# Three causal tiles in flight and context attention tile by tile in the first block, with interleaved queries in the second, of a four-block Perceiver kernel

## The chip, the core and the metric

One core of a Trainium2 chip runs the whole program. The metric is device microseconds of one execution, the median of the runs shown. Everything is float32. The engines are named as the profile names them: PE (TensorE matmul; PEld is its weight load), DVE (VectorE), ACT (ScalarE), POOL (GpSimd) and SP (SyncE, which issues most of the DMA transfers).

## The reference, cut to what matters

The network takes `x` (16 batches, 64 tokens, 256 features) and a context (16 batches, 1024 tokens, 192 features) through four blocks. Each block is a cross-attention on the context, a mixer over the tokens, and a feed-forward part, each added to `x` after a layer norm. The change touches the first block's first two parts and the second block's first part:

```python
x = x + L0_xattn(layernorm(x), ctx)      # one wide head: softmax(q k^T / 16) v, no output projection
x = x + L0_attn(layernorm(x), ...)       # rms-normed q, k; 16 heads of 16, causal over the 64 tokens
x = x + L0_ffn(layernorm(x), ...)        # top-2 of 8 experts, plus one shared expert
x = x + L1_xattn(layernorm(x), ctx)      # 16 heads of 16 on the context ("narrow heads")
...
```

## The kernel before, in words

The 1024 tokens are 8 tiles of 128 (two batches each), held in `xs`. A tile framework puts the instructions of each engine in an order and places the waits; inside `manual_schedule(engines={PE})` the PE's instructions keep the order in which the Python code emits them. The engines run their own lists in order, so an instruction that waits holds up all that stands behind it on its engine.

**First block, `L0_first`.** Per tile `i`, `scores(i)` multiplies queries that already carry the key weights (`qp`) with the transposed context (`ctxT`) of two batches into a PSUM tile `sc` of two banks; `exp_rows` takes the row maximum on DVE (`nmx`, L223) and the exponential on ACT (`p`, L225). `keys_first` turns `p` round on the PE (`ps_t`, L235) and copies it to `pT`. `averaged` multiplies `pT` with the context tokens (`ctx`, L349) and divides (`on`, L250). `by_features` transposes the result (L359, L360, copies `onT`), and `output` multiplies by the value weights (`misc<-w,onT`) and adds to `xs`. These run as a software pipeline over three iterations of the loop `for n in range(NT + 2)`: in iteration `n` the scores are those of tile `n`, the transposes and averages those of tile `n-1`, the output that of tile `n-2`.

Between these pieces stand nine calls of `attn.go()` per iteration. Each call advances the generators of `causal_attention`: every causal tile that is in flight (two at most) does its next piece, and so does the first routing generator in the list `behind`. A causal tile has 19 yields, many of them empty pieces that only leave time. In order its pieces are: the norm of `xs` (`os`); its transposes (`hTs`); the q, k, v matmuls (`misc<-w,hTs`) with the rms norm; transposes of q and k (`pt`, L717); scores of all heads (`sc<-w`), whose two PSUM tiles take both `sc` buffers, the mask (`sm`, L741), maxima (`mx`), a subtraction on POOL (L748), `exp` (L749), sums (L750); transposes of the exponentials (`pt`, L756); the products with v (`o`, L778, again in an `sc` buffer); the spreading of the sums' reciprocals (`misc<-rT,sel`); the projection (`misc<-w,yT`). A causal tile may start only once the context output of its tokens is in `xs` (`attn.ready`). After two causal tiles their routing for the experts follows. When the loop ends, `attn.go()` is called until all is done, with one piece of the shared expert (`shared_part`, tiles `gu` and `hid`) after each call.

The PSUM tags of this block are `sc` (2 buffers of two banks), `t` (2 of one bank) and `misc` (2 of one bank). Four context buffers hold two tiles' context. Transfers stand in SP's queue in program order; a transfer into a buffer that is still read holds up those behind it. The rooms of the two causal tiles in flight are carved from one slot of a ring of weight buffers.

**Second block, `L1_xattn`.** Per batch `keys_values(b)` gives four pieces (two of keys, two of values); `queries(i)`, in three turns, fetches for one tile of tokens the outputs of their two experts from memory (`carry`: two gathers on POOL, L1375, and two additions on DVE, L1384), normalizes (`ln_rs` on POOL, L160; `o`, L886), transposes, and multiplies, and copies the queries to a second layout by DMA (`qs<-qs`). Steps `(b, g)` then each do the scores, exponentials, transposes and averages of four heads (two score tiles of 128 rows: two heads times 64 queries), the transposes and averages one step behind the scores. Before, a block with PE and DVE in written order does the four pieces of batch 0 and then all of `queries(0)` and `queries(1)`, ahead of the first step:

```python
for piece in keys_values(0):
    piece()
for i in range(2):
    for _ in queries(i):
        pass
```

Of the kernel before, what the change touches and what calls it, by code (L numbers as in the profile page):

```python
# [21 lines left out]
NT = T // 128  # L22
# [20 lines left out]
class Net:  # L43
# [227 lines left out]
    def pack_L0_room(self):  # L271


        self.slot()
        return [
            (
                self.carve(128, 2, 2, 2 * S), self.carve(128, 2, 128), self.carve(128, D), self.carve(128, 2, D),
                self.carve(128, 2, 8, S), [self.carve(128, 4, 128) for _ in range(2)],
            )
            for _ in range(2)  # L280
        ]

    def L0_first(self):
# [5 lines left out]
        self.spare_dve = True  # L289
        self.tag, self.tag_bufs = "t", 2  # L290
        self.more_ctx(self.lp)
        self.norm_x()
# [9 lines left out]
        with self.tc.manual_schedule(engines={mybir.EngineType.PE}):  # L302
# [21 lines left out]
            def scores(i):  # L324
                ctx = ctxs.pop(i) if i in ctxs else fetch(i)
                if i == 2:
                    self.gate_w = self.load("L0f_gateT")
                    self.shared = tuple(self.load(f"L0f_{n}") for n in ("sw1", "sw3", "sw2"))
                sc = self.lps.tile([128, KEYS], F32, tag="sc", bufs=2, name="sc")

                for kh in range(2):
                    keys = bass.ts(kh, 512)
                    for ch in range(2):
                        for par in range(2):
                            b = 2 * i + par
                            nc.tensor.matmul(
                                sc[64 * par : 64 * par + 64, keys], qp[: HC + ch, ch, b * S : (b + 1) * S],
                                ctx[par][0][: HC + ch, ch, keys], start=ch == 0, stop=ch == 1,
                            )
# [30 lines left out]

            held = tail = None
            for n in range(NT + 2):
                got = (n, *scores(n)) if n < NT else None
                attn.go()
                if tail is not None:
                    onT = by_features(tail[1])
                attn.go()
                if held is not None:
                    i, ctx, sums, p = held
                    pT = self.keys_first(p, attn.go)  # L380
                attn.go()
                if tail is not None:
                    output(tail[0], onT)
                    attn.ready = tail[0] + 1
                attn.go()
                tail = None
                if held is not None:
                    tail = i, averaged(i, ctx, sums, pT)
                attn.go()
                attn.go()  # L390
                held = got
            del self.ctxT[2:], self.ctx[2:]
# [270 lines left out]
    def causal_attention(self, wqkv, wproj):  # L663
# [23 lines left out]
        def tile(i):  # L687
            if not rooms:
                rooms.extend(self.pack(ahead=False))
            qs, kT, v, qk, p16, p16T = rooms[i % 2]  # L690
            qs = qs.rearrange("p c b (h q) -> p c b h q", h=2)
            o = normalized(i, sb.tile([128, D], F32, tag="os", bufs=2, name="os"))
            yield
            yield
            hT = sb.tile([128, 2, 128], F32, tag="hTs", bufs=2, name="hTs")
            self.evict(hT, self.transposed(o))
# [3 lines left out]
            self.mm(ps.rearrange("p a b -> p (a b)"), [(hT[:, c, :], wqkv[:, c, :512]) for c in range(2)])  # L700
            sq = sb.tile([128, D], F32, tag="sq", bufs=2, name="sq")
            ss = self.small.tile([128, 2], F32, name="ss")
# [34 lines left out]

            sums = sb.tile([128, 2, 8], F32, tag="sums", bufs=2, name="sums")
            for jp in range(2):
# [21 lines left out]

            r = sb.tile([128, 2, 8], F32, tag="r", bufs=2, name="r")
            nc.vector.reciprocal(
# [4 lines left out]
            for b in range(2):  # L768
                nc.tensor.transpose(pr[:, b, :], r[:, b, :], self.ident)
            rT = sb.tile([8, 2, 128], F32, tag="rT", bufs=2, name="rT")  # L770
            nc.scalar.copy(rT, pr)
# [11 lines left out]
            o = o[:, :, : 4 * S].rearrange("p r (c n) -> p r c n", c=2)  # L783
            ym = sb.tile([128, 2, 2, S], F32, tag="ym", bufs=2, name="ym")
            nc.vector.tensor_scalar(ym, o[:, :, :, :S], own[:, 0:1], None, ALU.mult)
# [6 lines left out]
            for c in range(2):  # L792
                self.mm(ps[:, c], [(sel[:, h, c, :], rT[:, :, 64 * h : 64 * h + 64]) for h in range(2)])
            yT = sb.tile([128, 2, 2, S], F32, tag="yT", bufs=2, name="yT")
            nc.vector.tensor_tensor(
# [34 lines left out]
        def go():  # L830

            if len(s.work) < 2 and s.next < s.ready:
                s.work.append(tile(s.next))
                s.next += 1
            for w in list(s.work):
                if next(w, s) is s:
                    s.work.remove(w)
            if s.behind and next(s.behind[0], s) is s:
                s.behind.pop(0)
            return s.work or s.next < NT or s.behind  # L840
# [8 lines left out]
    def L1_xattn(self):  # L849
# [160 lines left out]
        with self.tc.manual_schedule(engines={mybir.EngineType.PE, mybir.EngineType.DVE}):  # L1010
            biases()
            for piece in keys_values(0):
                piece()
            for i in range(2):
                for _ in queries(i):
                    pass
        with self.tc.manual_schedule(engines={mybir.EngineType.PE}):
            held, work = None, {}
            steps = [(b, g) for b in range(B) for g in range(4)]
            for k in range(len(steps) + 4):  # L1020
# [5 lines left out]
                if k < len(steps):  # L1026
                    b, g = steps[k]
                    if not g:
                        sums = self.lp.tile([128, 8], F32, tag="sums", bufs=3, name="sums")
                        more = keys_values(b + 1) if b + 1 < B else None  # L1030
                    now = (b, g, scores(b, g, sums), sums)
                for piece in work.pop((k, "early"), ()):
                    piece()
                if k < len(steps):
                    if not b % 2 and not g and b // 2 + 2 < NT:
                        ahead = queries(b // 2 + 2)
                    if more is not None:
                        more[g]()
                    if b % 2 == 0 and g < 3 and b // 2 + 2 < NT:
                        next(ahead)  # L1040
# [170 lines left out]
    def shared_part(self, k):  # L1211
# [3 lines left out]
        cols = bass.ts(k, CHUNK)  # L1215
        hid = self.lp.tile([128, 3, CHUNK], F32, tag="hid1", bufs=3, name="hid")
        for m in range(3):
# [14 lines left out]
    def L0_ffn(self):  # L1232
        nc = self.nc
        self.blocks(self.routed, L0_BLOCKS)
        self.tag, self.tag_bufs = "gu", 4
        for k in range(2, NC):
            for _ in self.shared_part(k):
# [1255 lines left out]
```

## Time and profile before

| | before |
|---|---|
| median of 3 runs | 2849.67 us (2848.07 to 2859.1) |
| profiled execution | 2852.74 us, its span 2851.0 us |
| mean granted TensorE clock | 0.959 |
| busy share of the span | PE 92%, PEld 66%, DVE 49%, ACT 35%, POOL 11% |
| first scores of the first block to its last routing matmul | 31.46 to 273.68 us |
| second block's first matmul to its first turned exponentials | 440.18 to 484.25 us |

A page of the profile gives busy time by engine, slices of the span, the chain of work that ended last, the groups of instructions by line, and the waits. The trace answers the same for any stretch of time; "the windows" are a table with one row for each stretch: its length, the busy time of PE, PEld, DVE, ACT and POOL with numbers of instructions, the granted clock, the busy share of the DMA engines and their GB/s. In a timeline a row is start, duration, engine, line, operation, tiles, count, and in brackets the idle time before it with what ended it. Line 69 is the helper `mm`, line 64 the helper `evict`: there the tiles tell which call it is. One matmul of the program is two rows in the trace, since the count of float32 matmuls in the profile is twice that of the code.

### The profile page before, as it was taken

The numbers are of one execution on the slowest core, as the hardware profiler recorded it, in microseconds if no ns is written. First come the engines' busy times: TensorE is split into PE (matmuls) and PEld (weight loads), VectorE is DVE, ScalarE is ACT, GpSimd is POOL, SyncE is SP. The second block draws the span as 40 slices with busy tenths as digits, with TensorE's granted clock in tenths as the row PEclk, the third lists the DMA queues.
The fourth block names the chain that finished last, engine by engine and source line by source line (L and its number), as shares of the span: only waits on it lengthen the run. The fifth ranks groups of instructions, "written<-read, shape, count | busy, mean of one in ns | idle before, by whom it ended". The sixth has DMA issues, their size and how long they took to land.

```text
span 2851.0 us, 44735 instructions
## 1 busy us (share of the span) xinstructions
PE 2610.3 (92%) x18116; PEld 1892.4 (66%) x18116; DVE 1400.3 (49%) x2825; ACT 998.3 (35%) x2110; POOL 312.8 (11%) x429
## 2 busy tenths in 40 slices
PE   7887997999999898979999999698999998998999
PEld 3556894666666586856666676596666566666777
DVE  2655224666666653233434342422344756658692
ACT  1322222555555441222322322122234545454330
POOL 1111333000000011310101000201001000000000
PEclk9987997999999997989999999799999999999999
DMA  8611871110010113811111111463112213121210
GB/s 239 177 50 63 340 279 53 34 35 27 27 38 23 42 38 135 313 54 49 47 54 56 58 49 56 175 239 112 52 49 88 87 49 97 56 75 30 60 45 8
DMA packets 79228, 253.71 MB, mean 89 GB/s; under 512 B 15151, under 2 KB 26954, under 8 KB 69290
## 3 DMA queue, kind: packets, MB, share of 16 engines
q1 hardware_dynamic: 59562, 165.01, 18.3%
q0 software_dynamic: 13312, 80.28, 7.8%
q10 hardware_dynamic: 6144, 5.51, 0.6%
q8 instruction: 145, 2.38, 0.3%
q14 instruction: 65, 0.53, 0.1%
HBM read 233.80 MB, written 14.82 MB: 87 GB/s over the span
## 4 chain that ended last, share of the span: by engine, by line
PE 38%; DVE 9%; ACT 3%; issue 3%; DMA 2%; POOL 1%; SPq 1%; DVEq 0%; POOLq 0%; ACTq 0%
PE sc L501 9%; PE ps_h L69 4%; PE misc L537 4%; PE halves L69 3%; PE misc L69 3%; PE ps_t L515 3%; PE halves L537 3%; PE misc L532 2%; PE gu L69 2%; DVE x L2093 2%; PE halves L2117 2%; PE halves L532 1%; DVE nmx L223 1%; DVE x L2089 1%; DMA rep<-dus 1%
## 5 line engine op out<-in xcount | busy, mean ns | idle before, releaser
L223 DVE TENSOR_REDUCE nmx<-sc 128x1 f32<-128x1024 f32 x264 | 311.7, 1218 | 236.0 <-PE sc L501 146.1
L225 ACT ACTIVATE p<-sc,nmx 128x1024 f32<-128x1024 f32 x264 | 294.3, 1115 | 323.2 <-DVE nmx L223 323.0
L501 PE MATMUL sc<-ctxT,qp 128*128 128x512 f32 (+1 forms) x1024 | 358.3, 604 | 0.0
L501 PEld LDWEIGHTS sc<-ctxT,qp 128*128 128x128 f32 (+1 forms) x1024 | 139.8, 190 | 155.6 <-issue 153.2
L515 PE MATMUL ps_t<-ident,p 128*128 128x128 f32 x1024 | 140.9, 280 | 39.5 <-ACT pT L518 17.0
L2083 ACT ACTIVATE da<-rep,al 128x252 f32<-128x252 f32 x256 | 115.9, 500 | 134.0 <-DVE x L2093 123.8
L515 PEld LDWEIGHTS ps_t<-ident,p 128*128 128x128 f32 x1024 | 115.9, 143 | 64.3 <-ACT pT L518 20.2
L2093 DVE TENSOR_TENSOR_SCAN x<-da,x 128x512 f32<-128x512 f32 x128 | 152.7, 1218 | 2.7 <-ACT da L2083 1.9
L235 PE MATMUL misc<-ident,p 128*128 128x128 f32 x1024 | 137.1, 279 | 9.1 <-ACT p L225 6.3
L518 ACT COPY pT<-ps_t 128x512 f32<-128x512 f32 x166 | 94.2, 587 | 122.1 <-PE ps_t L515 117.1
L235 PEld LDWEIGHTS misc<-ident,p 128*128 128x128 f32 x1024 | 110.1, 141 | 34.8 <-ACT p L225 14.2
L160 POOL TENSOR_TENSOR ln_rs<-ln_ve,nhalf 128x1 f32<-128x1 f32 x80 | 45.1, 571 | 698.0 <-DVE ln_ve L158 605.3
L537 PE MATMUL halves<-pT,ctx 128*128 128x256 f32 x512 | 119.7, 387 | 0.0
L537 PE MATMUL misc<-pT,ctx 128*128 128x256 f32 x512 | 119.1, 386 | 0.0
L2089 DVE TENSOR_TENSOR x<-rep,bc_rep 128x512 f32<-128x512 f32 x128 | 84.6, 687 | 59.9 <-PE halves L2117 57.1
L237 ACT COPY pT<-misc 128x512 f32<-128x512 f32 x128 | 75.0, 586 | 109.7 <-PE misc L235 109.3
L69 PE MATMUL ps_h<-r,w 128*128 128x256 f32 x512 | 113.4, 381 | 0.0
L239 DVE COPY pT<-misc 128x512 f32<-128x512 f32 x128 | 88.3, 690 | 40.3 <-PE misc L235 28.8
L69 PEld LDWEIGHTS ps_h<-r,w 128*128 128x128 f32 x512 | 96.6, 190 | 15.9 <-issue 2.5
L537 PEld LDWEIGHTS halves<-pT,ctx 128*128 128x128 f32 x512 | 95.1, 191 | 17.4 <-issue 5.6
L537 PEld LDWEIGHTS misc<-pT,ctx 128*128 128x128 f32 x512 | 94.6, 190 | 17.1 <-issue 5.5
L69 PE MATMUL po<-wb,hid 128*128 128x256 f32 x440 | 100.3, 379 | 0.0
(500 smaller groups left out, 4502.4 us busy)
## 6 DMA issues: line engine op xcount, KB each, us to landing
ctx<-in_ctx SPq DMA_DIRECT2D x48, 768.0 KB, 4.4
ctxT<-in_ctxT SPq DMA_DIRECT2D x48, 512.0 KB, 3.3
w<-in_L2f_W SPq DMA_DIRECT2D x24, 1024.0 KB, 8.0
rep<-dus SPq DMA_DIRECT2D x256, 64.0 KB, 2.0
ctxT<-in_ctxT SPq DMA_DIRECT2D x16, 768.0 KB, 12.3
ctxT<-in_ctxT SPq DMA_DIRECT2D x96, 128.0 KB, 3.2
ys<-yb ACTq DMA_DIRECT2D x40, 128.0 KB, 7.2
bc_rep<-bcs SPq DMA_DIRECT2D x32, 128.0 KB, 2.9
```

The source lines that it names most:

```text
L69: self.nc.tensor.matmul(out, lhsT, rhs, start=n == 0, stop=n == len(pairs) - 1)
L223: self.nc.vector.tensor_reduce(nmx, sc, AX.X, ALU.max, negate=True)
L225: self.nc.scalar.activation(p, sc, AF.Exp, bias=nmx, accum_out=sums)
L235: self.nc.tensor.transpose(ps[:, u, :], p[:, at : at + 128], self.ident)
L239: self.nc.vector.tensor_copy(pT[:, 0:4, :], ps)
L501: nc.tensor.matmul(sc[u][:, bass.ts(kh, 512)], qp[n][par][rows, h : h + 2, :].rearrange("p h q -> p (h q)"), ctx[0][rows, at], start=n == ...
L515: nc.tensor.transpose(ps[:, t, :], p[:, at : at + 128], self.ident)
L518: nc.scalar.copy(to, ps)
L537: nc.tensor.matmul(o, ck[:, t, :128], pT[:, t].rearrange("p u q -> p (u q)"), start=t == 0, stop=t == NK - 1)
L2083: nc.scalar.activation(da[:, g, :, 1:], now[j][:, 0, :].rearrange("p (b s) -> p b s", s=S)[:, :, 1:], AF.Exp, scale=al[:, col : col + 1],)
L2089: nc.vector.tensor_tensor(h, now[j][:, 1:2, :].to_broadcast([128, 2, CHUNK]), bc[:, 0, states, :], ALU.mult)
L2093: nc.vector.tensor_tensor_scan(flat, da.rearrange("p g b s -> p (g b s)"), flat, 0.0, ALU.mult, ALU.add)
```

## The change

1. `L0_first` runs a tile's context attention from scores to output within one iteration `i`, with eight iterations in place of ten; nine `attn.go()` calls stand between the pieces as before. A tile's causal part may start in the last call of its own iteration.
2. Up to three causal tiles are in flight. Their rooms are made to fit by sharing memory: `qk` lies in the place of the later exponentials `p16`, and `qs` and `kT` in that of their transposes `p16T`. The small tiles get three buffers.
3. The transfers of tile `i + 2` are emitted after the averages of tile `i` (before: ahead of the scores of `i + 2`), those of the shared expert's weights after tile 0's. The shared expert's hidden tile takes the buffers of `pT` while in this block.
4. In `L1_xattn` the turns of `queries(0)` go between the four pieces of batch 0. `queries(1)` and `queries(2)` go turn by turn into the four steps of batch 0, and the first step does two pieces of batch 1's keys and values, the next two one each, the fourth none.

```diff
@@ pack_L0_room
+        for _ in range(3):
+            p16 = self.carve(128, 2, 8, S)
+            qk = p16[:, 0].rearrange("p n k -> p (n k)").rearrange("p (a d) -> p a d", d=D)
+            p16T = self.carve(128, 2, 4, 128)
+            early = p16T.rearrange("p j n q -> p (j n q)")
+            qs = early[:, :512].rearrange("p (c b q) -> p c b q", c=2, b=2)
+            kT = early[:, 512:768].rearrange("p (c q) -> p c q", c=2)
+            rooms.append((qs, kT, self.carve(128, D), qk, p16, [p16T[:, j] for j in range(2)]))
@@ L0_first
-            held = tail = None
-            for n in range(NT + 2):
-                got = (n, *scores(n)) if n < NT else None
-                attn.go()
-                if tail is not None:
-                    onT = by_features(tail[1])
-                attn.go()
-                if held is not None:
-                    i, ctx, sums, p = held
-                    pT = self.keys_first(p, attn.go)
-                attn.go()
-                if tail is not None:
-                    output(tail[0], onT)
-                    attn.ready = tail[0] + 1
-                attn.go()
-                tail = None
-                if held is not None:
-                    tail = i, averaged(i, ctx, sums, pT)
+            for i in range(NT):
+                ctx, sums, p = scores(i)
                 attn.go()
                 attn.go()
-                held = got
+                pT = self.keys_first(p, attn.go)
+                attn.go()
+                on = averaged(i, ctx, sums, pT)
+                if i + 2 < NT:
+                    ctxs[i + 2] = fetch(i + 2)
+                if not i:
+                    self.gate_w = self.load("L0f_gateT")
+                    self.shared = tuple(self.load(f"L0f_{n}") for n in ("sw1", "sw3", "sw2"))
+                attn.go()
+                onT = by_features(on)
+                attn.go()
+                output(i, onT)
+                attn.ready = i + 1
+                attn.go()
@@ causal_attention
-            qs, kT, v, qk, p16, p16T = rooms[i % 2]
+            qs, kT, v, qk, p16, p16T = rooms[i % 3]
...
-            if len(s.work) < 2 and s.next < s.ready:
+            if len(s.work) < 3 and s.next < s.ready:
@@ L1_xattn
-            for piece in keys_values(0):
+            for piece, turn in zip(keys_values(0), (None, *[queries(0)] * 3)):
                 piece()
-            for i in range(2):
-                for _ in queries(i):
-                    pass
+                if turn is not None:
+                    next(turn)
...
+            one, two = queries(1), queries(2)
+            ahead = (one,), (one, two), (one, two), (two,)
...
+                    if not k:
+                        more.pop(0)()
...
-                    if more is not None:
-                        more[g]()
+                    if more:
+                        more.pop(0)()
+                    if not b:
+                        for turn in ahead[g]:
+                            next(turn)
```

More of the change, by code (lines that the diff above doesn't have):

```diff
@@ L274, in pack_L0_room @@
         self.slot()
[L275 to L281, printed above, removed]
+        rooms = []
+        for _ in range(3):
[6 more added lines that the diff above has]
+            rooms.append((qs, kT, self.carve(128, D), qk, p16, [p16T[:, j] for j in range(2)]))
+        return rooms
     def L0_first(self):
@@ L290, in L0_first @@
         self.tag, self.tag_bufs = "t", 2
+        self.hid_tag, self.hid_bufs = "pT", self.n_pT
         self.more_ctx(self.lp)
@@ L324, in scores @@
             def scores(i):
[L325 to L328, printed above, removed]
+                ctx = ctxs.pop(i)
                 sc = self.lps.tile([128, KEYS], F32, tag="sc", bufs=2, name="sc")
@@ L689, in tile @@
                 rooms.extend(self.pack(ahead=False))
-            qs, kT, v, qk, p16, p16T = rooms[i % 2]
+            qs, kT, v, qk, p16, p16T = rooms[i % 3]
             qs = qs.rearrange("p c b (h q) -> p c b h q", h=2)
-            o = normalized(i, sb.tile([128, D], F32, tag="os", bufs=2, name="os"))
+            o = normalized(i, sb.tile([128, D], F32, tag="os", bufs=3, name="os"))
             yield
             yield
-            hT = sb.tile([128, 2, 128], F32, tag="hTs", bufs=2, name="hTs")
+            hT = sb.tile([128, 2, 128], F32, tag="hTs", bufs=3, name="hTs")
             self.evict(hT, self.transposed(o))
@@ L700, in tile @@
             self.mm(ps.rearrange("p a b -> p (a b)"), [(hT[:, c, :], wqkv[:, c, :512]) for c in range(2)])
-            sq = sb.tile([128, D], F32, tag="sq", bufs=2, name="sq")
+            sq = sb.tile([128, D], F32, tag="sq", bufs=3, name="sq")
             ss = self.small.tile([128, 2], F32, name="ss")
@@ L736, in tile @@
                         )
-            sums = sb.tile([128, 2, 8], F32, tag="sums", bufs=2, name="sums")
+            sums = sb.tile([128, 2, 8], F32, tag="sums", bufs=3, name="sums")
             for jp in range(2):
@@ L760, in tile @@
                 yield
-            r = sb.tile([128, 2, 8], F32, tag="r", bufs=2, name="r")
+            r = sb.tile([128, 2, 8], F32, tag="r", bufs=3, name="r")
             nc.vector.reciprocal(
@@ L769, in tile @@
                 nc.tensor.transpose(pr[:, b, :], r[:, b, :], self.ident)
-            rT = sb.tile([8, 2, 128], F32, tag="rT", bufs=2, name="rT")
+            rT = sb.tile([8, 2, 128], F32, tag="rT", bufs=3, name="rT")
             nc.scalar.copy(rT, pr)
@@ L783, in tile @@
             o = o[:, :, : 4 * S].rearrange("p r (c n) -> p r c n", c=2)
-            ym = sb.tile([128, 2, 2, S], F32, tag="ym", bufs=2, name="ym")
+            ym = sb.tile([128, 2, 2, S], F32, tag="ym", bufs=3, name="ym")
             nc.vector.tensor_scalar(ym, o[:, :, :, :S], own[:, 0:1], None, ALU.mult)
@@ L793, in tile @@
                 self.mm(ps[:, c], [(sel[:, h, c, :], rT[:, :, 64 * h : 64 * h + 64]) for h in range(2)])
-            yT = sb.tile([128, 2, 2, S], F32, tag="yT", bufs=2, name="yT")
+            yT = sb.tile([128, 2, 2, S], F32, tag="yT", bufs=3, name="yT")
             nc.vector.tensor_tensor(
@@ L1034, in L1_xattn @@
                 if k < len(steps):
-                    if not b % 2 and not g and b // 2 + 2 < NT:
-                        ahead = queries(b // 2 + 2)
-                    if more is not None:
-                        more[g]()
-                    if b % 2 == 0 and g < 3 and b // 2 + 2 < NT:
+                    if more:
[3 more added lines that the diff above has]
+                            next(turn)
+                    elif b % 2 == 0 and g < 3 and b // 2 + 2 < NT:
+                        if not g:
+                            ahead = queries(b // 2 + 2)
                         next(ahead)
@@ L1215, in shared_part @@
         cols = bass.ts(k, CHUNK)
-        hid = self.lp.tile([128, 3, CHUNK], F32, tag="hid1", bufs=3, name="hid")
+        hid = self.lp.tile([128, 3, CHUNK], F32, tag=self.hid_tag, bufs=self.hid_bufs, name="hid")
         for m in range(3):
@@ L1235, in L0_ffn @@
         self.tag, self.tag_bufs = "gu", 4
+        self.hid_tag, self.hid_bufs = "hid1", 3
         for k in range(2, NC):
```

## The prediction

> **What bounds the kernel now.** I read the page's busy shares first, then a table of windows over the two places that the change touches, then the waits there, then timelines.
>
> ```profile
> PE 2610.3 (92%) x18116; PEld 1892.4 (66%) x18116; DVE 1400.3 (49%) x2825; ACT 998.3 (35%) x2110; POOL 312.8 (11%) x429
> ```
>
> PE is busy 92% overall, so little is to be had in most stages. The windows show where it is not:
>
> ```profile
> 47.76:81.38 33.62, 28.05 (x176) 14.18 (x176) 11.61 (x27) 7.45 (x19) 4.04 (x7) 0.87 0.92 261
> 145.28:193.73 48.45, 42.76 (x338) 27.42 (x338) 28.17 (x101) 13.52 (x36) 7.76 (x11) 0.86 0.14 51
> 193.73:244.90 51.17, 42.82 (x296) 32.96 (x296) 28.42 (x98) 17.26 (x37) 6.64 (x9) 0.83 0.02 6
> 244.90:273.68 28.78, 20.60 (x111) 15.82 (x111) 14.78 (x60) 5.60 (x11) 3.33 (x5) 0.73 0.26 83
> 440.18:484.25 44.07, 32.30 (x91) 14.89 (x91) 17.99 (x46) 6.91 (x11) 19.91 (x25) 0.67 0.26 71
> ```
>
> The first block's loop ends near 193.7; after it come some 80 us of drain at clock 0.83 and 0.73 (rows three and four). The opening of the second block (last row) leaves PE idle for 11.8 of 44.1 us and runs it at 0.67. DMA is nearly full only at the start (0.92). No other engine is above 60% of any window; what holds PE are chains of waits:
>
> ```profile
> PE pt L756 <- ACT w L749: 13.6, 5, 4.6
> PE misc L179 <- DVE o L886: 10.0, 2, 5.1
> ```
>
> So `causal_attention`'s way from scores through mask, maxima, subtraction and exponential to its transposes costs PE 13.6 us in five waits, and two waits for the normalized tokens of `queries` cost 10.0 us. PE's timeline puts the second pair in place:
>
> ```profile
> 457.92 1.14 PE L943 MATMUL misc<-w,ctxT 64*128 64x256 f32 x8
> 464.00 0.66 PE L179 MATMUL misc<-ident,o 128*128 128x128 f32 x2 [4.95 <-DVE o L886]
> 475.17 0.66 PE L179 MATMUL misc<-ident,o 128*128 128x128 f32 x2 [5.08 <-DVE o L886]
> 484.25 0.66 PE L235 MATMUL misc<-ident,p 128*128 128x128 f32 x4
> ```
>
> **First block: the steady step.** I lay out one new step by hand, from the end O of `output(i)`, with the rows of 74 to 102 us, taken from start to start, at full clock. PE does `misc<-w,yT` and the causal `sc<-w` of tile i-1 until O+1.9. These take both `sc` buffers, so `scores(i+1)` now stands behind the masking `sm`, and all of PE behind it. DVE gets to `sm` after two additions of 0.42, the norm (0.43, 0.17, 0.15), POOL's power 0.55 and `os` 0.41: its first half ends at O+3.4, and PE has idled 1.5. `scores` 3.9, `os` transposes 0.4 and the first causal transposes bring O+8.2. DVE does the two `sums` (0.69 each) ahead of `nmx`, which then takes 1.22 and the exponential 1.12: `ps_t` starts at O+10.5, and PE has idled 2.3. Then, start to start: `ps_t` 0.59, `pt` 0.50, `misc<-w,hTs` 2.67, `ps_t` 0.47, averages 2.75, `r` 0.31, `o` 0.60, `rT,sel` 1.08, `pt` 0.49, `by_features` 0.41, the wait for `onT` about 0.6, `output` 1.03: 11.5, so O+22.0, of which PE idles 4.4. I add 0.8 for half-clock stretches (below): 22.8.
>
> Steps 4 and 6 also carry the routing of two tiles: 2.85 of PE, 1.9 by which `htok` and POOL's power delay the DVE's `nmx`, and waits on the routing's own chain. Before, those waits in the drain were 1.62, 0.47, 0.83 and 1.68 (4.6 together); with three tiles in flight I take 2.9. That makes 30.5 each.
>
> **First block: the sum.** First scores 31.46; `scores`, `nmx`, `exp`, `ps_t`, averages and output in a row are 12.6, so O(0) is 44.1. Step 1 is the same with 3.2 of tile 0's projections and a little waiting: O(1) is 60.2. Six steps follow, four plain, two with routing; step 2 lacks one `yT` (0.9): 60.2 + 4×22.8 + 2×30.5 − 0.9 = 211.5. Causal scores of tile 6 end at 213.4, against 218.75 before. But before had by then done about 11 us of the shared expert (`gu` and `hid` between 199.75 and 223), which now lies behind. To the last causal scores it took before 26.1 us; now the PE pieces there are 26.6 and the first routing wait, no longer covered by a second tile's pieces, 4.5: 244.5. The tail was 28.8; 13.7 us of it ran at half clock, and more `gu` to fill it should save 2.2: 271.0 against 273.68. The first block therefore brings about **−2.7 us**, far less than a loop two iterations shorter suggests: the drain loses six calls, but every step now holds a chain from scores to output that the old software pipeline spread over three.
>
> Smaller edits I cost at nothing, each for a cover. The transfers of tile i+2 go out after the averages of tile i, the same moment at which their buffers come free before; 3 MB a tile at the 261 GB/s of row one are about 12 us, below 16.1 and 22.8 a step. If that cover failed, the price is row 47.76's wait for `ctxT`, 5.1 us, once. Shared rooms: `p16` is written after `qk`'s transposes, `p16T` after the scores that read `qs` and `kT`, so order alone covers them. `hid` in `pT`'s buffers: the last reader, the averages of tile 7, is past.
>
> **The clock.** Gaps of 1.5 and 2.3 lie near where this trace's clock goes either way:
>
> ```profile
> 80.80 0.66 PE L756 MATMUL pt<-ident,w 128*128 128x128 f32 x4 [1.92 <-ACT w L749]
> 145.28 7.04 PE L336 MATMUL sc<-ctxT,qp 96*64 96x512 f32 x16 [2.00 <-DVE sm L741]
> 100.81 1.04 PE L756 MATMUL pt<-ident,w 128*128 128x128 f32 x4 [3.02 <-ACT w L749]
> 145.30:152.10 6.80, 6.80 (x16) 1.70 (x16) 3.09 (x5) 1.26 (x2) 2.04 (x2) 0.50 0.27 103
> 74.00:100.80 26.80, 21.86 (x228) 14.45 (x228) 16.09 (x40) 8.22 (x20) 6.25 (x9) 1.00 0.83 219
> ```
>
> The first gap left the clock at 1.00 (last row). The second, hardly longer, was followed by 6.8 us at 0.50, in which the scores took 7.0 instead of 3.9; half of 6.8 is lost, 3.4. The third was followed by 3.4 us at half clock (100.9 to 104.3), 1.7 lost. One such stretch in two to four steps is my 0.8 a step; the bounds are 0 and, with both gaps caught, 2×3.4 = 6.8.
>
> The Trainium skill, page "TensorE: Matmul & The Clock Gate", section "HAM oscillation — how this bites in real kernels", speaks of idle gaps above some 3.4 us as the ones to avoid. By it gaps of 1.5 and 2.3 us would be free and the first block 5 us better than I say; the 2.00 us gap above, followed by half clock, is against that, so I keep the row.
>
> **Second block.** Before, PE ended batch 0's keys and values at 459.06 and waited 4.95 for `o`, since POOL did tile 0's power only at 462.81, behind gathers; then 5.08 more for `queries(1)`; the clock was 0.50 from 462.7 to 483.2. Now `queries(0)` is emitted among the four pieces, `queries(1)` after the first scores. In the built order of POOL eleven gathers stand ahead of tile 0's power; at 1.25 a gather (465.00 to 466.39 and 469.26 to 473.02 in the trace), with waits for free buffers, the power comes at about 458.4, the transposes of `o` at 459.5 (before 464.66). PE idles about 3.3 there instead of 4.95. Then queries 1.1, values 3.1, the second layout of `qs` by DMA (about 2, beside values), batch 1's first piece 3.1, scores 2.1 at half clock, `nmx` 1.22 and `exp` 1.12: first turned exponentials at 472 to 474.6 against 484.25, −11. By then 3.1 more of keys and values is done and 1.5 less of `queries(1)`: −12.6. Some 2.2 of idle near 493 goes as well; about 2 are lost where the fourth step has no piece of keys to fill it. I take **−12**, bounds −8 (POOL's power as late as 462.8, nothing gained on the first wait) and −14.
>
> Together −14.7: 2838.0 against the profiled 2852.74. The median of the runs lies 3.1 below the profiled execution, so **2835**.
>
> **Rivals.** *Full gain*: DVE's order is the scheduler's, and if `nmx` goes ahead of `sums` and the mask is done earlier, half of the idle goes: plain steps 20.0, routing steps 26.0, −(4×2.8 + 2×4.5) = −20 more: 2815. For it: before's steps are no longer than 24.7 for a tile, at DVE 74% (window 120.56 to 145.28). Against: `sums` can start 1.3 earlier than `nmx`. *Second block alone*: a step grows by about 2 (DVE in the steps with routing), the first block gives back 10: 2845 to 2848, no measurable change. *Slower*: both gaps of each step trip the half clock as at 145.28; 6.8 in place of 0.8, +6 a step over six steps is +36: 2835 + 36 = 2871. For it: that row, and clock 0.83 in the drain; against: 1.92 left the clock alone. It decides from about 4.8 a step above my sum, where the step is 27.6 and the time 2864. That the change doesn't do what it says I give nothing: the built orders show three tiles and the interleaved queries.
>
> **How the numbers follow.** About 0.5%, 14.2 us, is what a measurement of this kernel can tell from no change: faster means below 2835.4, slower above 2863.9. Forecast 0.45, its own range 2823 to 2845 (bounds of the second block +4/−2, of the routing waits ±3, of the clock ±5), 0.27 of it below the limit as the unknown waits there are partly covered, 0.18 above. Full gain 0.23, second block alone 0.18, slower 0.14. So faster 0.50, same 0.36, slower 0.14. The range reaches from 2812 (full gain and a little) to 2856, leaving out the slower case and little of the full gain.
>
> **What would show it.** Right: `output` matmuls 22 to 24 apart in plain steps, near 30 in two; the last one near 211; `route_seen` near 271; the first turned exponentials of the second block near 473, with one wait for `o` of about 3 in place of two of 5. Wrong: steps above 27 with a mean clock below 0.8; PE waiting for `ctxT` again; transposes of `o` still at 464; or steps of 20.

## The result, and the profile after

The changed kernel is slower, by little: median 2860.39 us (2851.0 to 2869.16, 20 runs) against 2850.97 us (20 runs) for the kernel before on the same chip; ratio 1.0025, 95% interval 1.0015 to 1.0034, some 7 us (the two medians lie 9.4 apart). Run once more on another chip, it stood at 1.0034 (1.0021 to 1.0048). The forecast was 2835, with a range from 2812 to 2856: it said faster, and the measured median lies above the range. The profiled execution after took 2858.44 us, its span 2856.7 us.

The page's busy shares after, as in the prediction's first fence, hardly differ; the extra time is idle:

```profile
PE 2609.4 (91%) x18116; PEld 1892.9 (66%) x18116; DVE 1400.8 (49%) x2825; ACT 1001.8 (35%) x2112; POOL 311.8 (11%) x429
```

The windows after are cut at the start of `output` (`misc<-w,onT`) of one tile and the next, so that the first five rows are steps 2 to 6; then the drain to the last causal scores, the tail to `route_seen`, and the opening of the second block to its first turned exponentials. Columns: stretch, length, busy time of PE, PEld, DVE, ACT, POOL, granted clock, DMA share, GB/s.

```profile
61.19:84.12 22.93, 18.23 (x158) 10.65 (x158) 10.65 (x24) 7.09 (x18) 3.39 (x5) 0.93 0.53 153
84.12:108.95 24.83, 20.77 (x163) 12.54 (x163) 10.96 (x25) 7.19 (x18) 3.39 (x5) 0.86 0.44 129
108.95:143.13 34.18, 27.93 (x186) 17.54 (x186) 18.96 (x76) 8.23 (x22) 4.47 (x7) 0.77 0.42 132
143.13:169.05 25.92, 21.00 (x164) 13.36 (x163) 11.15 (x26) 7.02 (x16) 3.39 (x5) 0.84 0.32 79
169.05:198.99 29.94, 22.32 (x186) 14.08 (x186) 18.90 (x77) 8.13 (x22) 4.37 (x6) 0.94 0.41 137
...
221.33:259.35 38.02, 32.09 (x225) 24.70 (x225) 21.34 (x84) 15.77 (x29) 4.37 (x6) 0.91 0.02 8
259.35:284.19 24.84, 18.21 (x123) 14.29 (x122) 15.39 (x63) 5.58 (x11) 3.40 (x5) 0.93 0.28 96
...
450.27:489.55 39.28, 32.68 (x97) 15.96 (x97) 20.93 (x57) 7.59 (x12) 22.62 (x29) 0.74 0.28 82
```

PE is idle for 4 to 8 us of each step, and the clock differs from step to step (0.77 to 0.94 here, 1.00 in step 7, which took 22.3). PE's waits in the first block after (us in total, times, longest):

```profile
PE ps_t L235 <- ACT p L225: 17.3, 8, 2.7
...
PE sc L337 <- DVE sm L739: 10.1, 6, 2.1
PE misc L69 <- DVE t_both L1118: 6.3, 3, 2.2
PE misc L69 <- DVE onT L363: 4.3, 6, 0.8
```

The 13.6 us that PE waited for `w L749` are gone (2.6 left), and in their place stand the waits of one tile's own chain: for its exponentials, for the mask that frees `sc`, for `onT`. On PE's timeline:

```profile
65.44 5.36 PE L337 MATMUL sc<-ctxT,qp 96*64 96x512 f32 x16 [2.07 <-DVE sm L739]
...
73.38 0.66 PE L235 MATMUL ps_t<-ident,p 128*128 128x128 f32 x4 [1.78 <-ACT p L225]
...
113.91 6.90 PE L337 MATMUL sc<-ctxT,qp 96*64 96x512 f32 x16 [1.91 <-DVE sm L739]
...
203.46 3.66 PE L337 MATMUL sc<-ctxT,qp 96*64 96x512 f32 x16 [1.41 <-DVE sm L739]
...
284.19 0.60 PE L69 MATMUL misc<-route_seen,ones 128*128 128x8 f32 x2
...
469.70 0.66 PE L179 MATMUL misc<-ident,o 128*128 128x128 f32 x2 [4.72 <-DVE o L884]
470.15 3.62 PE L934 MATMUL misc<-w,ctxT 128*128 128x256 f32 x8
...
482.21 2.04 PE L69 MATMUL sc<-kT,qs 32*128 32x512 f32 x4 [1.60 <-DMA qs<-qs]
```

The context scores, 3.66 at full clock (step 7, at 203.46), take 5.36 and 6.90 behind gaps of 2.07 and 1.91. `route_seen` comes at 284.19 in place of 273.68, and the second block's first matmul at 450.27 in place of 440.18. Its steady steps then come only 2.5 us later than before (scores that stood at 712.2 at 714.8), so the second block gained 7.6. The prediction's −2.7 and −12 are therefore +10.5 and −7.6 in these two profiles. What lies behind differs by 3 us more, in code that the change does not touch.

### The profile page after: what moved, and what is told of

The parts are those of the page before. It is cut to its first block, busy times and chain, and to the rows that moved or that the text cites. A ratio compares the mean times of both kernels' runs of the same rounds, so it can differ in the third digit from the quotient of the medians.

```text
span 2856.7 us, 44741 instructions
## 1 busy us (share of the span) xinstructions
PE 2609.4 (91%) x18116; PEld 1892.9 (66%) x18116; DVE 1400.8 (49%) x2825; ACT 1001.8 (35%) x2112; POOL 311.8 (11%) x429
## 4 chain that ended last, share of the span: by engine, by line
PE 38%; DVE 9%; ACT 3%; issue 2%; DMA 2%; POOL 1%; SPq 1%; DVEq 0%; ACTq 0%; POOLq 0%
PE sc L499 9%; PE ps_h L69 4%; PE misc L535 4%; PE halves L69 3%; PE misc L69 3%; PE ps_t L513 3%; PE halves L535 3%; PE misc L530 2%; PE gu L69 2%; DVE x L2098 2%; PE halves L2122 2%; PE halves L530 1%; DVE nmx L223 1%; DVE x L2094 1%; DMA rep<-dus 1%
## 5 line engine op out<-in xcount | busy, mean ns | idle before, releaser
L239 DVE COPY pT<-misc 128x512 f32<-128x512 f32 x128 | 88.1, 689 | 39.9 <-PE misc L235 28.8
```

The lines of the kernel that those rows point to most:

```text
L239: self.nc.vector.tensor_copy(pT[:, 0:4, :], ps)
```

## The experiments

Ratios are to the kernel before on the same chip, with 95% intervals; the first block's end is `route_seen` in the profiled execution.

| kernel | ratio | `route_seen` |
|---|---|---|
| before; again | 1 | 273.7; 268.8 |
| the change; again | 1.0025 (1.0015–1.0034); 1.0034 (1.0021–1.0048) | 284.2; 284.1 |
| second block's part alone | 0.9972 (0.9961–0.9983) | 275.4; 269.5 |
| first block's part alone | 1.0048 (1.0030–1.0065) | 284.8 |
| change, gaps partly filled; again | 1.0010 (1.0001–1.0019); 1.0010 (0.9999–1.0021) | 273.3; 274.1 |
| change, gaps filled | 1.0011 (1.0001–1.0021) | 277.4 |
| change, two in flight | 1.0039 (1.0023–1.0054) | 295.7 |
| change, causal scores a call earlier | 1.0030 (1.0019–1.0042) | 287.3 |
| change, a call ahead of `keys_first` | 0.9966 (0.9954–0.9979) | 271.8 |
| both | 0.9956 (0.9940–0.9972) | 267.0 |
| a call ahead, one gap partly filled | 0.9951 (0.9935–0.9967) | 261.9 |
| a call ahead, two gaps filled | 0.9946 (0.9932–0.9961) | 258.2 |
| old loop, three in flight, new second block | 0.9952 (0.9936–0.9968) | 267.8 |
| the same, values first | 0.9955 (0.9941–0.9969) | 267.2 |
| second part, values first | 0.9981 (0.9972–0.9990) | 274.1 |
| second part, wait filled | 0.9979 (0.9968–0.9991) | 267.9 |

### The two parts, each alone

```diff
 # kernel before
-    def L1_xattn(self):   # of before
+    def L1_xattn(self):   # of the change
```

> The kernel before with the second block's new order alone. In the two profiles the second block's start lies 10.1 us later after the change, and its steady steps only 2.5 us later, so the second block gained 7.6 us of the 12 forecast. If the two parts are independent: 2850.97 - 7.6 = 2843, and route_seen stays at 273.7. If the gain came only from the first block's late end (its DMA or POOL work already done by then), the time stays at 2849 to 2852.

Measured: 0.9972, some 8 us faster. From the block's first matmul to its steady steps it took 7.3 us less than before.

```diff
 # changed kernel
-    def L1_xattn(self):   # of the change
+    def L1_xattn(self):   # of before
```

> The change with the second block of before. Independent parts: route_seen near 284, the second block's start 10 later than before, the time 2860 to 2868. If the half clock in the first block is a toss of the gaps' lengths, route_seen moves by some us from run to run around that.

Measured: 1.0048, some 14 us slower, `route_seen` at 284.8, steady steps of the second block 10.0 late. The parts are independent within the intervals (−8 + 14 = +6, measured +7 to +10): the whole loss is the first block's.

### Idle gaps filled with matmuls that nobody reads

```diff
             for i in range(NT):
+                if i > 1:
+                    ps = self.room_t([128, 4, 128])
+                    for u in range(5):
+                        nc.tensor.transpose(ps[:, u % 4, :], self.ident, self.ident)
                 ctx, sums, p = scores(i)
 # keys_first, first half, ahead of the transposes of p:
+            for u in range(6):
+                self.nc.tensor.transpose(ps[:, u % 4, :], self.ident, self.ident)
```

> The change, with PE's two idle gaps of each step filled by transposes of the identity that nobody reads (five ahead of the scores from tile 2 on, six ahead of the first transposes of the exponentials): same work, same chains, no idle there. Clock theory: the granted clock of the steps, 0.77 to 1.00 now, goes to nearly 1.00; by the clock alone 61.2 to 221.3 loses 18.9 us (each step's length times one minus its clock), so route_seen comes at 266 to 272 and the time falls to 2843 to 2849. Chain theory (the waits for exponentials, mask and output in a row are what is lost): the steps stay within 3 us of now and the time at 2855 to 2865.

Two windows of it, a plain step and the six steps together, and its waits:

```profile
83.20:105.50 22.30, 18.77 (x174) 12.20 (x173) 10.89 (x26) 7.20 (x17) 3.39 (x5) 1.00 0.51 147
...
61.00:212.40 151.40, 122.96 (x1074) 81.69 (x1070) 81.58 (x254) 45.89 (x109) 22.30 (x32) 0.97 0.40 119
```

```profile
PE ps_t L237 <- ACT p L225: 16.0, 8, 2.4
...
PE sc L339 <- DVE sm L745: 6.0, 6, 1.4
```

With 0.8 us of idle work in each gap, and gaps of up to 1.4 and 2.4 left, the steps' clock is 0.97, plain steps are 22.1 to 22.9, and `route_seen` comes 10.9 earlier. So a part of the loss is the clock's, and it is what the forecast's step left out: the six steps take 151.4 in place of 160.1. Yet the times fell only from 1.0025 or 1.0034 to 1.0010, 4 to 7 us, to a median of 2857.9 where the clock theory had 2843 to 2849: this profiled execution was the fastest of its twelve, 7 below their median. Hence the further runs:

```diff
-                    for u in range(5):
+                    for u in range(12):
-            for u in range(6):
+            for u in range(16):
 # output, ahead of its matmuls:
+                for u in range(5):
+                    nc.tensor.transpose(po[:, u % 2 * 128 : u % 2 * 128 + 128], self.ident, self.ident)
```

> The change with its idle gaps filled nearly whole by transposes of the identity that nobody reads: twelve (1.5 us) ahead of the context scores, sixteen (2.1 us) ahead of the transposes of the exponentials, five (0.65 us) ahead of output. PE then has no gap above 0.7 in a plain step, and the chains are as long as before. Clock theory: the granted clock of every step is near 1.00, the time falls by the 14 us that the half clock took beyond the forecast's 0.8 a step: ratio to before 0.997 to 0.999. Chain theory: the steps stay 22.3 and over, the routing's steps 28 and over, and the time falls by no more than the 4 us that the first filling brought: 1.0005 to 1.0015.

Measured: 1.0011, the same as with the smaller filling; the plain steps run at clock 1.00 and are 22.3 to 22.5 long, the two routing steps 31.9 each at 0.89, the drain is longer, and `route_seen` comes at 277.4. Filling more gives nothing more, as the chain theory had it: a step at full clock is still 22 us, since its chain is as long whatever PE does in the gaps.

The first filling again, and the change again, unaltered:

> The first filling (0.8 us in each of two gaps) once more, on this chip. Its profiled execution was the fastest of twelve. If the 10.9 us that its profile gained on the change in the first block were that execution's luck, route_seen now lies at 277 to 284; if they are the filling's, at 271 to 276, and what its times lack lies behind the first block.

> The changed kernel once more, on the chip of the next runs, as their measure: ratio to before 1.0025 as in its first twenty runs. The profile tells how far the first block's clock is a matter of luck: route_seen 284.2 in the first profile; if the half-clock stretches fall differently from run to run, it moves by over 3 us and with it the granted clock between 60 and 222 us (0.77 to 1.00 by step).

Measured: 274.1 and 284.1, and 1.0010 and 1.0034. The first block's times in the profile repeat for these two kernels to within 1 us; the difference between 4 to 7 us in the medians and 10 in the profile is not luck of one profile. Where the rest is lost in the other runs was not found.

### The profile of before, again

> The kernel before, profiled once more. Its only profile so far has route_seen at 273.7 and clocks of 0.73 to 1.00 in the first block; the kernel with the second part alone, whose first block is the same, had 275.4 in an execution that was the slowest of its twelve. If the half-clock stretches there are a matter of one execution, route_seen now differs by over 4 us; if they repeat as those of the change did (284.2, 284.1), it lies at 273 to 276.

```profile
145.09 3.66 PE L336 MATMUL sc<-ctxT,qp 96*64 96x512 f32 x16 [2.00 <-DVE sm L741]
...
268.75 0.59 PE L69 MATMUL misc<-route_seen,ones 128*128 128x8 f32 x2 [0.37 <-DVE route_table L1186]
```

Two windows of it, the drain (from the end of the last `output` to the end of the last causal scores) and the tail (from there to `route_seen`):

```profile
188.93:239.96 51.03, 42.27 (x296) 32.26 (x296) 28.41 (x98) 17.24 (x37) 6.63 (x9) 0.87 0.02 6
239.96:268.75 28.79, 20.62 (x112) 15.83 (x110) 14.78 (x60) 5.59 (x11) 3.33 (x5) 0.73 0.25 83
```

> The kernel with the second part alone, profiled once more: same question for the same first block (275.4 then), and for the gain of the second block (steady steps 7.3 us earlier against the block's start than before): within 1.5 of 7.3 if it is the order's, further off if the clock between 460 and 482 decides it.

Measured: 268.8 for the kernel before and 269.5 with the second part. With the two experiments on the second block below (274.1 and 267.9), the first block of before thus ends anywhere from 267.9 to 275.4 in six profiles, and the one that the forecast was summed against (273.7) lies in the later half. Against the two of this section the change's first block is 15 us behind, not 10.5. The second block's gain was 7.3 again.

All of this spread arises in the loop. In the six profiles the last `output` starts anywhere from 186.9 to 194.2, while the drain takes 51.0 to 51.4 and the tail 28.8 every time. One place in the loop is in the prediction's own rows on the clock: the scores of 145.28, 7.04 long behind a gap of 2.00, take 3.66 here behind a gap of the same 2.00. The length of that gap does not settle which clock follows it.

### Two in flight

```diff
-            if len(s.work) < 3 and s.next < s.ready:
+            if len(s.work) < 2 and s.next < s.ready:
```

> The change with two causal tiles in flight, as before, in place of three. If the third tile in flight is what crowds DVE and makes the steps long, steps shorten and route_seen comes before 284. If it is needed by a loop of nine calls per tile and twenty calls per causal tile, the tiles pile up behind the loop: each of the later tiles starts one or two calls later, some 8 calls in all, and the drain grows by 10 to 20 us: 2868 to 2880.

```profile
PE ps_t L235 <- ACT p L225: 10.6, 6, 2.6
...
PE pt L754 <- ACT w L747: 10.3, 4, 4.7
```

Measured: 1.0039 and `route_seen` at 295.7. The old wait (`pt` for `w`, 10.3) comes back beside the new one. The six steps take as long as with three in flight (160.6 against 160.1), and from the last `output` to `route_seen` it takes 71.9 in place of 62.9. So the third tile in flight is no cause of the loss; without it the drain grows. In the times this is not shown: 1.0039 lies within the interval of the change's second measurement.

### The causal scores a call earlier

```diff
 # causal_attention, ahead of the scores: two empty pieces
-            yield
             yield
 # behind the scores
-            for _ in range(3):
+            for _ in range(4):
                 yield
```

> The change with the causal scores one call earlier (one empty piece moved from ahead of them to behind them), so that they stand between by_features and output, and the mask is done while PE does output and the projection. Chain theory: of each step's idle the gap ahead of the context scores (1.4 to 2.1) and the wait for onT (0.8) go, a wait of some 0.6 for the copied queries and keys may come; 1.6 to 2.3 a step over six steps, 10 to 14 us, and less half clock on top: route_seen 262 to 273, the time 2838 to 2852. If the half clock is set by the other gap (ahead of the transposes of the exponentials, 1.8 to 2.7) alone, the clock of the steps stays near 0.86 and only the 10 us come.

```profile
69.80 0.69 PE L179 MATMUL misc<-ident,os 128*128 128x128 f32 x2 [2.58 <-DVE os L682]
70.28 1.06 PE L753 MATMUL pt<-ident,w 128*128 128x128 f32 x4
```

Measured: 1.0030, `route_seen` at 287.3: no gain. The wait ahead of the scores is gone, but DVE now does the mask and the maxima first, so that the next tile's `os` is late and PE waits for it behind the scores (2.58). The gap was turned into another, followed by half clock again (`pt` 1.06 in place of 0.60).

### A call ahead of keys_first

```diff
-                pT = self.keys_first(p, attn.go)
+                attn.go()
+                pT = self.keys_first(p)
                 attn.go()
```

> The change with one call of the causal pieces moved from between the two halves of keys_first to ahead of it, so that 3.3 us of causal matmuls fill the gap ahead of the transposes of the exponentials (1.8 to 2.7 a step, 17.3 in all). Against it: the averages then follow the second half's copy (0.6) with nothing between. Chain theory: 1.2 to 2.1 a step over seven steps, 8 to 15 us; clock theory: the other gap of 1.4 to 2.1 alone is shorter than any that tripped the clock in the plain steps, so the clock rises to near 1.00 and 10 more us come. route_seen 260 to 275.

PE's waits and the steps' window:

```profile
PE sc L337 <- DVE sm L740: 8.9, 6, 2.1
...
PE ps_t L235 <- ACT p L225: 2.6, 1, 2.6
```

```profile
58.00:208.00 150.00, 130.16 (x1017) 78.54 (x1017) 81.84 (x253) 44.14 (x109) 22.34 (x32) 0.85 0.42 127
```

Measured: 0.9966, 17 to 19 us faster than the change in the times, 12.4 in the profile. The wait for the exponentials fell from 17.3 to 2.6: PE's own causal work stands in it. The clock did not rise (0.85): it is not this gap alone that trips it. The expectation was also wrong to hold the other gap too short for that: in the change, scores at 88.59 took 5.35 behind a gap of 1.42. So most of this gain is the wait itself. This one reordering removes the change's loss in the first block.

> Both of these. If the change loses through the idle of its steps, they fall to 19 to 20.5 us (plain) and 25 to 27 (routing), the last output comes near 200 in place of 222 and route_seen near 255 to 262; the time 2826 to 2842, faster than both kernels. If DVE's order or the routing's chain takes over as the limit, plain steps stay above 21.

Measured with the last two edits together: 0.9956, `route_seen` 267.0, later than expected (255 to 262). One plain step took 20.3 (from 82.98 to 103.26 between causal scores), as expected; the other three took 21.0 to 23.2, the two with routing 27.9 and 28.1. The wait for `os` and one for the copied keys (7.6 in seven times) stay.

```diff
 # a call ahead of keys_first, and in the loop:
+                if i > 1:
+                    ps = self.room_t([128, 4, 128])
+                    for u in range(8):
+                        nc.tensor.transpose(ps[:, u % 4, :], self.ident, self.ident)
                 ctx, sums, p = scores(i)
```

> The kernel with the call moved ahead of keys_first (the gap ahead of the transposes of the exponentials filled with causal work), and eight transposes of the identity that nobody reads, 1.0 us, in the gap ahead of the context scores (1.4 to 2.1, from tile 2 on). Clock theory: that kernel still ran at 0.83 between 100 and 200 us, with only this gap and the waits for onT and routing left, so plain steps fall to 20 and route_seen from 271.8 to 262 to 267. If what trips the clock there is the routing's waits (t_both, s_col, 2 to 2.8), the clock of 100 to 200 stays below 0.88 and route_seen within 3 of 271.8.

> The kernel with the call ahead of keys_first, with twelve transposes of the identity (1.5 us) ahead of the context scores and five (0.65 us) ahead of output: a candidate for the best. Clock theory: route_seen 258 to 263, time 0.994 to 0.995 of before, at or below the 0.9951 of the smaller filling. If the filling only takes PE time that the chain then lacks, 0.995 to 0.997.

Measured: 0.9951 and 0.9946, `route_seen` 261.9 and 258.2. The window of the second, cut at its outputs:

```profile
57.98:196.06 138.08, 123.92 (x1119) 82.70 (x1120) 81.37 (x253) 43.65 (x109) 22.34 (x32) 0.99 0.46 135
```

With the longer gap taken by real work and the others filled, six steps take 138 us in place of 160 and run at 0.99. This is the lowest ratio of all, some 15 us below before; the intervals of the next ones (0.9951 to 0.9956) overlap with its own. Nobody reads what its idle transposes write.

### The old loop with three tiles in flight

```diff
 # changed kernel, with L0_first of before and in it:
+        self.hid_tag, self.hid_bufs = "pT", self.n_pT
```

> The change with the first block's loop of before (a tile's context attention over three iterations), but three causal tiles in flight and their shared rooms, and the second block of the change. It tells the loop from the third tile in flight. If the loop is what costs, route_seen lies within 5 of the 273.7 of before (three tiles in flight save calls of the drain: a tile starts every nine calls and lasts twenty) or up to 10 earlier, and the time is that of the second block's part alone or better, 2833 to 2848. If it is the third tile's pieces that lengthen the way of each tile, route_seen comes after 278.

Measured: 0.9952, `route_seen` 267.8, at best 1 us earlier than the two earliest of the six profiles of before's first block (267.9 and 268.8), and `pt` waits for `w` 6.5 us in place of 13.6; the second block gained 10.9 here. With the same rooms, the same three tiles and the same second block as the change, the old loop is 21 to 23 us faster in the times (0.9952 against 1.0025 or 1.0034): the loop, not the third tile, is what the change loses by. (With the old loop the transfers go back to their old place; that does not explain the difference, since here PE waits 6.2 for `ctxT` and in the change not at all.) The third tile, added to the kernel with the second part alone (0.9972), brings some 6 in the times, but the two intervals overlap and the profiles of the first block do not show it.

### The second block

```diff
-            for piece, turn in zip(keys_values(0), (None, *[queries(0)] * 3)):
-                piece()
-                if turn is not None:
-                    next(turn)
+            turn = queries(0)
+            for n, piece in enumerate(keys_values(0)):
+                piece()
+                if n == 1:
+                    next(turn)
+            next(turn)
+            next(turn)
```

> The kernel before with the second block's new order, but batch 0's last piece (values, ready long before) ahead of the transposes of tile 0's normalized tokens, not behind them. PE waited there 4.9 with that piece queued behind. Order theory: PE does the 3.1 us of values in the wait, which falls to about 1.7; keys of batch 1 start 3 to 5 earlier (the piece ran at half clock, 5.4), and the steady steps come 3 to 5 earlier than with the second part alone: ratio to before 0.9955 to 0.996 in place of 0.9972. Rival: POOL's powers behind eleven gathers and the layout's DMA hold the first scores anyway, and what is saved ahead comes back as a wait for qs: within 1.

Measured: the wait for the transposes of `o` falls to 1.9, and from the block's start the steady steps come 9.4 earlier than before in place of 7.3; the times (0.9981 against 0.9972) show no gain. Together with three in flight in the old loop:

> Three causal tiles in flight in the loop of before, the second block's interleaving, and the values piece ahead of the transposes. If the three add: three in flight alone 273.7 - 267.8 = 6, the second block 8, the values 3 to 5: 17 to 19 below before, ratio 0.9933 to 0.994. If the values' piece gives nothing, 0.995 as without it.

Measured: 0.9955, no different from 0.9952 without it.

```diff
 # transposed(o) of queries(0), ahead of its transposes:
+        for u in range(24):
+            self.nc.tensor.transpose(ps[:, u % 2, :], self.ident, self.ident)
```

> The kernel before with the second block's new order and 24 transposes of the identity that nobody reads, 3 to 6 us, in the 4.9 us ahead of the same transposes: the wait as long as before, PE not idle in it. Clock theory: the clock between 462 and 482 (about 0.7 in the kernel with the second part alone) goes to nearly 1.00, the values piece takes 3.1 in place of 5.4, the next pieces 3.1 in place of 5.3, and the steady steps come 4 to 5 earlier. If the chain to the first scores decides (o, queries, layout DMA), they come at most 2 earlier.

```profile
454.85 0.44 PE L181 MATMUL misc<-ident,o 128*128 128x128 f32 x2 [1.95 <-DVE o L888]
455.12 1.94 PE L938 MATMUL misc<-w,ctxT 128*128 128x256 f32 x8
...
464.88 3.78 PE L924 MATMUL misc<-ctxT,w 128*128 128x512 f32 x4 [5.67 <-DVE v L62]
```

Measured: the 24 transposes take 2.8 and 1.95 of the wait is left; the values run at full clock (1.94 for what took 3.62), and then PE waits 5.67 for the copy of `v`, which stands on DVE behind additions that wait for gathers. The scores that stood at 712.2 before stand at 700.1, 12.1 earlier, of which the block's first matmul had 5.3 already: from the block's start the steady steps come 6.8 earlier, against 7.3 without the filling. The times (0.9979 against 0.9972) tell no difference. In this kernel the clock was therefore not what held the opening; what the faster values saved came back as the wait for DVE's queue behind POOL's gathers. The framework planned DVE's order anew around the added matmuls, so this reading does not carry over unchanged to the kernel without them.

## Why the prediction was wrong, point by point

**What held.** The hand-laid step was right where it spoke of chains: 22.0 at full clock, measured 22.3 to 22.5 (step 7, and the filled kernels); gaps of 1.5, 2.3 and 0.6 forecast, 1.42 to 2.07, 1.78 to 2.66 and 0.82 measured. That `sums` delay `nmx` held only where the scores run at full clock: in step 7 they end at 207.1, `sums` last until 208.1, and the gap is 2.66. Where part of the scores runs at half clock, `nmx` starts 0.1 behind them and the gap is 1.78, so that scores 1.7 longer cost the chain only 0.8 to 0.9. The edits costed at nothing cost nothing: after, the trace lists no wait of PE for `ctxT` in the first block. Before had two, 7.0 us together, so the new loop covers these, a gain that the sum holds without naming it. The tail (26.6) took 24.8.

**The term that failed in the sum: the clock.** I put 0.8 a step for it, 4.8 in six. The six steps took 160.1 where the sum has 151.3. With the gaps partly filled, and the chains as they were, they took 151.4, and 153.6 in the second profile of that kernel. So 6.5 to 8.7 us of the missing 8.8 are shown to be the clock's. The clocks themselves say more: the six steps' lengths times one minus their clocks make 18.9, 3.1 a step; but this counts half clock in stretches where PE waits for a chain anyway. "One such stretch in two to four steps" should have been nearly one a step (five of the six have one); the slower rival, whose mechanism this is, priced it at 6.8 a step. In the times the clock is worth 4 to 7 us.

**The rest of the first block.** Tiles 0 and 1 came 2.1 later than summed; the six steps took 8.8 more (the two with routing, 30.5 each in the sum, 34.2 and 29.9); the drain to the last causal scores took 3.9 more, the tail 1.8 less. Together 13.0, the distance from 271.0 to 284.2 but for rounding.

**The comparison that was missing.** A sum that meets the step does not tell whether the step is good: 22 us at full clock hold 4.4 of idle, mostly waits of a tile for its own exponentials, which the three-iteration loop had covered. I counted this idle and still expected a gain, since the sum was held against the end of one execution of before, and no step of the old loop was laid out beside the new one. One call of the causal pieces, moved, took 14.7 us of waits away and 17 to 19 us of time: more than the whole loss.

**The reference.** −2.7 was read against one execution of before with 273.7. Further profiles of the same first block have 267.9 to 275.4: up to 6 us of the error lie in the figure that the sum was compared with. The drain and the tail, which the prediction dwells on, repeat to 0.4 us; what belonged to that one execution was the loop.

**The second block.** −12 forecast, −7.3 to −7.6 in the profiles of these two kernels, some 8 in the times: the lower end of the stated bounds. The transposes of `o` came where they were forecast (19.4 after the block's first matmul; the 464.66 beside them in the prediction is the end of before's, which start at 464.00). But the wait ahead of them was 4.7, not 3.3, as PE arrived sooner; the values queued behind it ran at a clock of 0.51 (5.5, not 3.1); and the DMA of the second layout was no longer beside the values, since the queries' matmuls stand behind these: 1.6 of wait. The first turned exponentials came 39.3 after the block's first matmul, where the forecast had 33 and before 44.1.

**The rivals.** "Second block alone" was the nearest in kind: the first block gives back, only 14 in place of 10, so that the sum is above zero. By the prediction's own limits (slower above 2863.9) the result counts as no change, to which it gave 0.36.

The Trainium skill, page "TensorE: Matmul & The Clock Gate", section "HAM oscillation — how this bites in real kernels", warns of gaps above some 3.4 us. Here gaps of 1.91 and 2.07, with others near them, were followed by scores of 6.90 and 5.36 us in place of 3.66. The same page's section "A second HAM failure mode: psum-queue depth-cycling" says that frequent short idles can make the clock swing as well: this agrees with the steps at 0.77 to 0.94, and with 0.97 once 0.8 us of each gap were filled.

## What to carry to other kernels

When a loop is made shorter by doing a unit of work from end to end, list for each link of its chain which independent work stands on PE beside it; a link with nothing beside it costs its whole length in every step, and moving one piece there can be worth more than the restructuring. Sum against more than one execution of the kernel before: here its loop ended up to 7 us apart, while its drain and tail repeated to 0.4 us. A wait that is filled or moved comes back as the next one in the same engine's queue unless that queue is followed too (the mask ahead of `os`, the copy of `v` behind the gathers).

## What was not expected of the hardware

Steps with two gaps of 1.4 to 2.7 us each ran at a mean granted clock of 0.77 to 0.94, and one with gaps of 1.41 and 2.66 at 1.00. With 0.8 us of matmuls in each gap, and gaps up to 1.4 and 2.4 left, the six steps together ran at 0.97. The longer gap taken away alone left it at 0.85. The same gap of 2.00 ahead of the same scores was followed by 7.04 us of them in one execution of the same code and by 3.66 in another. And the first block's end repeated within 1 us in the profiles of the change and of its filled version, while that of before was found at 267.9 to 275.4, with its last 80 us the same each time.
